# Edge lists with room in steps of 32, list sums from signs, and attention sums divided on ScalarE, in a four-layer graph network

## The chip, the cores and the metric

One core of one Trainium2 chip. The metric is the device time of one execution in microseconds (us), the median of several. All runs compared were in the fast state of their chip (one of the 20 runs of x_less_pe0 was slow and is left out; f_before is a single run, whose state can't be told, but its 1780.26 us is within 0.3 us of the median of the 16 runs of the same kernel beside it, 1780.51). The chips themselves differ, though, and this matters throughout: the kernel before takes about 1780 us on some (called **quick chips** here) and 1940 to 1960 us on others (**slow chips**). So runs are compared only with runs of the kernel before on the same chip. A ratio is the mean time of one kernel's fast runs over that of the other's of the same rounds, so it is not quite the ratio of the medians that are quoted; brackets give its 95% interval.

## The reference

3327 nodes with 512 features, an adjacency matrix (ones with probability falling with both node numbers, so early rows are heavy), and four layers, each followed by a residual addition and a layer norm:

```python
x = _layernorm(x + _L0_gnn_ref(x, adj, W, a1, a2))       # graph attention, 8 heads of 64, softmax over neighbours, elu
x = _layernorm(x + _L1_gnn_ref(x, adj, ...))             # mean of the neighbours' x, three 512x512 products, relu
x = _layernorm(x + _L2_gnn_ref(x, adj, ...))             # mean of the first 64 neighbours, two products, leaky relu
x = _layernorm(x + _L3_gnn_ref(x, adj, W, a))            # attention, 4 heads of 128 (quaternion weights)
```

## The kernel before

The engines' names in the profiles: PE is TensorE's matmuls, PEld its weight loads, DVE VectorE, ACT ScalarE, POOL GpSimd. The kernel never multiplies with the dense matrix (apart from block 0 in the mean layers). It makes a list of the edges of each block of 128 nodes, in chunks of 128 edges. Each layer then gathers the source rows of a chunk with one indirect DMA issued by GpSimd (a **gather**; its rows land in a ring of buffers), and TensorE adds them into the block's sum with a 0/1 selection matrix. Cut to what the change touches:

```python
CAPS = (0, 19, 15, 13, 11, 10, 10, 9, 9, 8, 8, 7, 7, 7, ...)     # chunks of 128 per block's list
...
    step = const.tile([P, P], F32, name="step")                   # difference of neighbours, for the list sums
    nc.vector.tensor_copy(step, ident)
    nc.vector.tensor_sub(step[:, 1:], ident[:, 1:], ident[:, :P - 1])
...
                    u = mid.tile([P, g * P], BF16, name="u")      # list sums: place >= start, then a product with dl
                    nc.vector.tensor_scalar(u, place[:, c0 * P:(c0 + g) * P], start, None, ALU.is_ge)
...
    def gather(ring, table, l, c0, g):
        t = ring.take(g)
        for c in range(g):
            nc.gpsimd.indirect_dma_start(
                out=t[:, c, :], out_offset=None, in_=table[:, :],
                in_offset=bass.IndirectOffsetOnAxis(ap=l.idx[:, c0 + c:c0 + c + 1], axis=0))
        return t
...
            for c in range(g):                                    # attention layers 0 and 3, one group of chunks
                for s in range(2):
                    nc.tensor.matmul(accs[b][s], S[:, c, :], G[:, c, s * hh * M:(s + 1) * hh * M],
                                     start=at + c == 0, stop=at + c == chunks_of[b] - 1)
...
            for s in range(2):                                    # end of a block: attention sum / its weight
                nc.vector.tensor_mul(h[:, s], acc[s][:, :, :OUT], rden[:, s].to_broadcast([P, hh, OUT]))
...
            for k in range(3):                                    # mean layers 1 and 2: three bf16 parts of a row
                nc.tensor.matmul(accs[b], S[:m, c, :], G[:m, c, k * D:(k + 1) * D],
                                 start=at + c + k == 0, stop=k == 2 and at + c == n - 1)
```

## Time and profile before

| | us |
|---|---|
| time before, median of 3 runs (quick chip) | 1779.0 (1775.2 to 1780.38) |
| span of the profile of before that the prediction read | 1940.1, mean granted clock 0.927 |

The second row was on hand and I only scaled it away: the profile was of a slow chip (the profiled execution itself took 1941.98 us), the times of a quick one. The granted clock is the share of TensorE's full clock that the throttle let through. The prediction shows the profile's lines. A profile of the kernel before on a quick chip came with the experiments (run f_before, 1780.26 us), and it is the one to compare with the kernel after. Its first line of busy time and shares, then busy us (instructions) of PE, PEld, DVE, ACT, POOL by stage, granted clock, DMA share and GB/s. The stages are: before layer 0, layer 0, layer 1, block 0 of layer 2, the rest of layer 2, layer 3 without its first and last groups.

```profile
PE 1565.7 (88%) x8167; PEld 1027.4 (58%) x8215; DVE 1286.9 (72%) x3269; ACT 668.4 (38%) x1964; POOL 975.7 (55%) x1061
...
0.00:231.00 231.00, 183.73 (x1046) 136.00 (x1047) 189.22 (x693) 116.21 (x447) 24.79 (x37) 0.94 0.53 176
231.00:699.00 468.00, 430.54 (x2691) 312.55 (x2691) 435.23 (x1103) 245.38 (x585) 269.84 (x298) 0.95 0.73 232
699.00:1069.00 370.00, 367.08 (x1300) 173.70 (x1323) 211.49 (x429) 71.53 (x136) 223.35 (x230) 1.00 0.86 297
1069.00:1146.00 77.00, 69.83 (x228) 33.17 (x230) 34.32 (x60) 13.46 (x29) 21.56 (x29) 0.98 0.54 197
1146.00:1403.00 257.00, 234.06 (x1054) 141.01 (x1074) 127.90 (x312) 66.45 (x326) 194.12 (x193) 0.99 0.94 324
1430.00:1762.00 332.00, 261.10 (x1741) 217.56 (x1741) 272.46 (x616) 140.04 (x390) 238.92 (x272) 0.95 0.75 216
```

What to see, against the stages in the prediction: the instructions are the same (the trace of f_before lacks the records of 48 matmuls, 8167 against 8215), yet TensorE has far less idle time. In layer 1 it idles 3 of 370 us (18 to 21 of 394 to 397 in the slow chip's profile); over the whole span it idles 213 us against 314.

### The profile page before, as it was taken

The numbers are of one execution on the slowest core, as the hardware profiler recorded it, in microseconds if no ns is written. First come the engines' busy times: TensorE is split into PE (matmuls) and PEld (weight loads), VectorE is DVE, ScalarE is ACT, GpSimd is POOL, SyncE is SP. The second block draws the span as 40 slices with busy tenths as digits, with TensorE's granted clock in tenths as the row PEclk, the third lists the DMA queues.
The fourth block names the chain that finished last, engine by engine and source line by source line (L and its number), as shares of the span: only waits on it lengthen the run. The fifth ranks groups of instructions, "written<-read, shape, count | busy, mean of one in ns | idle before, by whom it ended". The sixth has DMA issues, their size and how long they took to land.

```text
span 1940.1 us, 25543 instructions
## 1 busy us (share of the span) xinstructions
PE 1626.2 (84%) x8215; PEld 1055.9 (54%) x8215; DVE 1286.1 (66%) x3269; ACT 666.7 (34%) x1964; POOL 970.9 (50%) x1061
## 2 busy tenths in 40 slices
PE   5999477888889999998899999688888568778775
PEld 4667366655566774443444444355555456566654
DVE  8897489988988883135567864633434336677887
ACT  3365344545544553211111121122222313333443
POOL 1000455544455643637665532666666266666660
PEclk9899688989999999999999999898898889898998
DMA  8434667766765757968888873888888366666771
GB/s 268 149 116 151 205 200 256 255 221 215 237 178 177 220 161 254 310 215 294 271 314 284 284 279 130 284 278 293 294 297 275 91 184 186 192 203 197 205 210 61
DMA packets 125148, 431.38 MB, mean 222 GB/s; under 512 B 25294, under 2 KB 26830, under 8 KB 125004
## 3 DMA queue, kind: packets, MB, share of 16 engines
q0 software_dynamic: 76480, 314.26, 52.1%
q1 hardware_dynamic: 48524, 115.40, 17.0%
q8 instruction: 67, 1.10, 0.2%
q14 instruction: 77, 0.63, 0.1%
HBM read 381.54 MB, written 48.04 MB: 221 GB/s over the span
## 4 chain that ended last, share of the span: by engine, by line
PE 61%; DVE 22%; issue 10%; DMA 2%; ACT 2%; another core or an unknown queue 2%; POOL 1%; SPq 0%; DVEq 0%; ACTq 0%; POOLq 0%
PE po L742 17%; PE acc L1077 15%; PE acc L1351 14%; PE po L965 7%; DVE gt L1070 4%; DVE cand L854 3%; PE pt L727 2%; PE pg L1050 2%; DMA gt<-t_d,idx 2%; DVE cand L868 1%; DVE sl L866 1%; DVE st L747 1%; DVE val L836 1%; DVE e L1099 1%
## 5 line engine op out<-in xcount | busy, mean ns | idle before, releaser
L934 POOL DMA_INDIRECT gt<-t_d,idx x788 | 788.3, 1000 | 726.9 <-ACT g0own L788 201.9
L1077 PE MATMUL acc<-gt,sel 128*128 128x264 f32 (+1 forms) x1828 | 484.4, 414 | 52.9 <-issue 26.1
L1077 PEld LDWEIGHTS acc<-gt,sel 128*128 128x128 f32 x1828 | 357.5, 203 | 139.4 <-issue 80.4
L1070 DVE TENSOR_TENSOR gt<-gt,pg 128x1536 f32<-128x1536 f32 (+1 forms) x137 | 263.2, 1921 | 10.7 <-ACT sel L1065 4.6
L742 PE MATMUL po<-wn,xt 128*128 128x512 f32 x416 | 201.5, 629 | 20.9 <-ACT xt L730 11.1
L934 POOL DMA_INDIRECT gx<-t_d,idx x116 | 116.5, 1004 | 63.1 <-issue 27.2
L965 PE MATMUL po<-w,xt 128*128 128x262 f32 x416 | 112.5, 431 | 36.1 <-issue 32.7
L742 PEld LDWEIGHTS po<-wn,xt 128*128 128x128 f32 x416 | 81.2, 202 | 110.3 <-issue 92.5
L1062 ACT ACTIVATE pg<-sc 128x24 f32<-128x24 f32 (+4 forms) x148 | 28.1, 190 | 301.1 <-DVE sc L1061 162.5
L1351 PE MATMUL acc<-gt,sall 128*128 128x512 bf16 x498 | 118.7, 388 | 8.4 <-issue 8.2
L854 DVE MAX8 cand<-val 128x8 f32<-128x832 uint16 (+40 forms) x259 | 125.6, 524 | 0.0
L965 PEld LDWEIGHTS po<-w,xt 128*128 128x128 f32 x416 | 88.2, 215 | 61.0 <-issue 38.5
L1050 PEld LDWEIGHTS <-ds 128*128 128x128 bf16 x1482 | 64.2, 99 | 92.6 <-issue 47.0
L1351 PE MATMUL acc<-gt,sel 128*128 128x512 bf16 x495 | 114.0, 379 | 0.0
L965 PE MATMUL po<-gt,xt 128*128 128x268 f32 x416 | 104.3, 400 | 2.8 <-ACT xt L734 2.6
L1351 PEld LDWEIGHTS <-sall 128*128 128x128 fp8e4 x615 | 61.1, 100 | 83.8 <-issue 22.0
L730 ACT COPY xt<-pt 128x512 f32<-128x512 f32 x86 | 50.6, 589 | 152.6 <-PE pt L727 90.3
L1351 PEld LDWEIGHTS <-sel 128*128 128x128 bf16 x615 | 60.2, 98 | 78.5 <-issue 17.3
L742 PE MATMUL po<-wx,xt 128*128 128x512 f32 x208 | 97.2, 610 | 5.6 <-issue 2.5
L1038 ACT ACTIVATE far<-place,nmid 128x384 int16<-128x384 int16 (+2 forms) x148 | 94.8, 644 | 20.4 <-DVE ds L1042 13.0
L727 PE MATMUL pt<-s_ident,xres 128*128 128x128 f32 x520 | 80.1, 278 | 21.2 <-DMA xres<-in_x_dram 16.0
L742 PE MATMUL po<-wl,xt 128*128 128x512 f32 x208 | 94.0, 594 | 2.9 <-issue 1.5
(230 smaller groups left out, 2465.6 us busy)
## 6 DMA issues: line engine op xcount, KB each, us to landing
ab<-in_adj_dram SPq DMA_DIRECT2D x25, 832.0 KB
ab<-in_adj_dram SPq DMA_DIRECT2D x25, 831.5 KB
t_d<-t SPq DMA_DIRECT2D x50, 384.0 KB
gt<-t_d POOLq DMA_DIRECT2D x42, 384.0 KB
gt<-t_d,idx POOLq DMA_INDIRECT x788
t_d<-tg SPq DMA_DIRECT2D x25, 264.0 KB
t_d<-tg SPq DMA_DIRECT2D x25, 260.0 KB
xres<-in_x_dram SPq DMA_DIRECT2D x25, 256.0 KB
```

The source lines that it names most:

```text
L727: nc.tensor.transpose(pt[:, c, :], src[:, c * P:(c + 1) * P], ident)
L730: nc.scalar.copy(xt, pt)
L742: nc.tensor.matmul(po, xt[:, c, :], w[:, c], start=c == 0, stop=c == DC - 1)
L854: nc.vector.max(out=top, in_=seg)
L934: nc.gpsimd.indirect_dma_start(out=t[:, c, :], out_offset=None, in_=table[:, :], in_offset=bass.IndirectOffsetOnAxis(ap=l.idx[:, c0 + c:c0 ...
L965: nc.tensor.matmul(pw[s], xt[:, c, :], self.w[:, c, s, :], start=c == 0, stop=c == DC - 1)
L1038: nc.scalar.activation(far[:, :g * P], place[:, c0 * P:(c0 + g) * P], AF.Abs, bias=l.nmid, scale=2.0)
L1050: nc.tensor.matmul(pe[:, c], ds[:, c * P:(c + 1) * P], self.own[:, k, :, b], start=k == 0, stop=k == 2)
L1062: nc.scalar.activation(w[:, :g], sc[:, :g, 0], AF.Exp)
L1070: nc.vector.tensor_mul(Gc[:, :, :OUT], Gc[:, :, :OUT], w[:, :g].rearrange("p c (h o) -> p (c h) o", o=1).to_broadcast([P, g * H, OUT]))
L1077: nc.tensor.matmul(accs[b][s], S[:, c, :], G[:, c, s * hh * M:(s + 1) * hh * M], start=at + c == 0, stop=at + c == chunks_of[b] - 1)
L1351: nc.tensor.matmul(accs[b], S[:m, c, :], G[:m, c, k * D:(k + 1) * D], start=at + c + k == 0, stop=k == 2 and at + c == n - 1)
```

## The change

Intent: (1) give each list room in multiples of 32 edges instead of 128, so that 4 of 247 chunks go and many last gathers bring 32, 64 or 96 rows; group sizes are fitted to the end of the ring; (2) take the comparison behind the list sums off VectorE by a sign activation on ScalarE; (3) do the division of the attention sums on ScalarE, head by head.

```diff
-CAPS = (0, 19, 15, 13, 11, 10, 10, 9, 9, 8, 8, 7, ...)
+CAPS = (0, 2368, 1856, 1568, 1376, 1280, 1152, 1088, 1024, 992, 928, 896, ...)
...
+        L = self.L = -(-room // P)
+    def places(self, c):
+        return min(P, self.room - c * P)
...
+    def ahead(self):                                  # class Ring
+        return self.parts[self.part].shape[1] - self.at
...
-    nc.vector.tensor_copy(step, ident)
-    nc.vector.tensor_sub(step[:, 1:], ident[:, 1:], ident[:, :P - 1])
+    nc.vector.tensor_scalar(step, ident, 0.5, None, ALU.mult)
+    nc.vector.scalar_tensor_tensor(step[:, 1:], ident[:, :P - 1], -0.5, step[:, 1:], ALU.mult, ALU.add)
+    nc.vector.scalar_tensor_tensor(step[:, 0:1], ident[:, P - 1:], 0.5, step[:, 0:1], ALU.mult, ALU.add)
...
+                nc.scalar.activation(here, p1[:, 0:1], AF.Identity, bias=point5, scale=-1.0)
...
-                    nc.vector.tensor_scalar(u, place[:, c0 * P:(c0 + g) * P], start, None, ALU.is_ge)
+                    nc.scalar.activation(u, place[:, c0 * P:(c0 + g) * P], AF.Sign, bias=here)
...
-                for k in range(n):
-                    g = l.L // n + (k < l.L % n)
+                while c0 < l.L:
+                    left = l.L - c0
+                    g = -(-left // -(-left // GROUP))
+                    if 1 < ring.ahead() < g:
+                        g = ring.ahead()
...
-                out=t[:, c, :], ... ap=l.idx[:, c0 + c:c0 + c + 1]
+                out=t[:m, c, :], ... ap=l.idx[:m, c0 + c:c0 + c + 1]          # m = l.places(c0 + c)
...
+            for p0 in range(m, P, 32):                # attention: zero the scores of rows not gathered
+                nc.scalar.copy(G[p0:p0 + 32, g - 1]...[:, :, OUT:], zeros[p0:p0 + 32, :2 * H]...)
...
-                    nc.tensor.matmul(accs[b][s], S[:, c, :], G[:, c, s * hh * M:(s + 1) * hh * M],
+                    nc.tensor.matmul(accs[b][s], S[:m, c, :], G[:m, c, s * hh * M:(s + 1) * hh * M],
...
-                nc.vector.tensor_mul(h[:, s], acc[s][:, :, :OUT], rden[:, s].to_broadcast([P, hh, OUT]))
+                for k in range(hh):
+                    nc.scalar.activation(h[:, s, k], acc[s][:, k, :OUT], AF.Identity, scale=rden[:, s, k])
```

Cut: the same for the heavy lists of block 0, the constants that the sign form needs, the arguments that pass the ring, the row counts in the mean layers.

More of the change, by code (lines that the diff above doesn't have):

```diff
@@ L524, in general_path @@
     gat("l3", xs_d[2], out, l3_w.shape[0], l3_w.shape[2], l3_weights, False)
-HEAVY = ((0, 9, 14, 120, 9, 3), (9, 18, 14, 120, 9, 3), (18, 27, 14, 120, 9, 3))
-CAPS = (0, 19, 15, 13, 11, 10, 10, 9, 9, 8, 8, 7, 7, 7, 7, 7, 6, 6, 6, 6, 6, 6, 6, 6, 5, 5)
+HEAVY = ((0, 9, 1760, 120, 9, 3), (9, 18, 1792, 120, 9, 3), (18, 27, 1792, 120, 9, 3))
+CAPS = (0, 2368, 1856, 1568, 1376, 1280, 1152, 1088, 1024, 992, 928, 896, 864, 832, 800, 768, 768, 736, 704,
+        704, 672, 672, 672, 640, 640, 608)
 SLOTS = (0, 48, 40, 40, 32, 32, 32, 32, 32) + (24,) * 17
@@ L544, with __init__ @@
 class EdgeList:
-    def __init__(self, pool, name, cuts, L, K, rounds, at):
-        self.cuts, self.L, self.K, self.rounds, self.at = cuts, L, K, rounds, at
+    def __init__(self, pool, name, cuts, room, K, rounds, at):
+        self.cuts, self.room, self.K, self.rounds, self.at = cuts, room, K, rounds, at
+        L = self.L = -(-room // P)
         self.idx = pool.tile([P, L], U32, name=f"idx{name}")
@@ L646, in sparse_path @@
         lists.append([])
-        for q, (s0, s1, L, K, n, rounds) in enumerate(parts):
+        for q, (s0, s1, room, K, n, rounds) in enumerate(parts):
             cuts = [int(NP * ((s0 + (s1 - s0) * s / n) / total) ** 2) // 2 * 2 for s in range(n + 1)]
             cuts = [c for i, c in enumerate(cuts) if i in (0, n) or c >= 8 * rounds]
-            lists[b].append(EdgeList(keep, f"{b}_{q}", cuts, L, K, rounds, sum(map(len, lists)) - 0))
+            lists[b].append(EdgeList(keep, f"{b}_{q}", cuts, room, K, rounds, sum(map(len, lists)) - 0))
     NL = sum(map(len, lists))
@@ L680, in sparse_path @@
     pos = iota("pos", LMAX, I16, P, 0, 1)
+    zeros = const.tile([P, 16], F32, name="zeros")
+    nc.gpsimd.memset(zeros, 0.0)
     eps = const.tile([P, 1], F32, name="s_eps")
@@ L692, in sparse_path @@
     step = const.tile([P, P], F32, name="step")
-    nc.vector.tensor_copy(step, ident)
-    nc.vector.tensor_sub(step[:, 1:], ident[:, 1:], ident[:, :P - 1])
+    nc.vector.tensor_scalar(step, ident, 0.5, None, ALU.mult)
+    nc.vector.scalar_tensor_tensor(step[:, 1:], ident[:, :P - 1], -0.5, step[:, 1:], ALU.mult, ALU.add)
+    nc.vector.scalar_tensor_tensor(step[:, 0:1], ident[:, P - 1:], 0.5, step[:, 0:1], ALU.mult, ALU.add)
     dls = [const.tile([P, 2, KMAX + 2], BF16, name=f"dl{k}") for k in range(2)]
     for dl in dls:
-        for s in range(2):
-            nc.gpsimd.memset(dl[:, s, 0:1], 1.0 - s)
+        nc.gpsimd.memset(dl[:, 0, 0:1], 0.5)
+        nc.gpsimd.memset(dl[0:1, 0, 0:1], 0.5 + P / 2)
+        nc.gpsimd.memset(dl[:, 1, 0:1], 0.0)
+    point5 = const.tile([P, 1], F32, name="point5")
+    nc.gpsimd.memset(point5, 0.5)
     H0, _, OUT0 = l0_w.shape
@@ L880, in structure @@
                 nc.tensor.matmul(p1[:, 1:2], middle, dg, start=True, stop=True)
+                here = mid.tile([P, 1], F32, name="here")
+                nc.scalar.activation(here, p1[:, 0:1], AF.Identity, bias=point5, scale=-1.0)
                 nc.scalar.copy(start, p1[:, 0:1])
@@ L916, in structure, with groups @@
             yield b
-    def groups(blocks=range(NB)):
+    def groups(ring, blocks=range(NB)):
         for b in blocks:
@@ L922, in groups @@
             for l in lists[b]:
-                n = -(-l.L // GROUP)
                 c0 = 0
-                for k in range(n):
-                    g = l.L // n + (k < l.L % n)
+                while c0 < l.L:
[3 more added lines that the diff above has]
+                        g = ring.ahead()
                     yield b, l, c0, g, at
@@ L933, in gather @@
         for c in range(g):
+            m = l.places(c0 + c)
             nc.gpsimd.indirect_dma_start(
-                out=t[:, c, :], out_offset=None, in_=table[:, :],
-                in_offset=bass.IndirectOffsetOnAxis(ap=l.idx[:, c0 + c:c0 + c + 1], axis=0))
+                out=t[:m, c, :], out_offset=None, in_=table[:, :],
+                in_offset=bass.IndirectOffsetOnAxis(ap=l.idx[:m, c0 + c:c0 + c + 1], axis=0))
         return t
@@ L1035, in group @@
             G = gather(ring, self.table, l, c0, g)
+            m = l.places(c0 + g - 1)
+            for p0 in range(m, P, 32):
+                nc.scalar.copy(G[p0:p0 + 32, g - 1].rearrange("p (h m) -> p h m", m=M)[:, :, OUT:],
+                               zeros[p0:p0 + 32, :2 * H].rearrange("p (h s) -> p h s", s=2))
             far = sp.tile([P, GROUP * P], I16, name="far")
@@ L1075, in group @@
             for c in range(g):
+                m = l.places(c0 + c)
                 for s in range(2):
-                    nc.tensor.matmul(accs[b][s], S[:, c, :], G[:, c, s * hh * M:(s + 1) * hh * M],
+                    nc.tensor.matmul(accs[b][s], S[:m, c, :], G[:m, c, s * hh * M:(s + 1) * hh * M],
                                      start=at + c == 0, stop=at + c == chunks_of[b] - 1)
@@ L1286, in sparse_path @@
     w2lay = ExitStack()
-    for item in groups():
+    for item in groups(pools[0]):
         b = item[0]
@@ L1348, in mean_group @@
         for c in range(g):
-            m = LAST if b == 0 and c0 + c == NB - 1 else P
+            m = LAST if b == 0 and c0 + c == NB - 1 else P if b == 0 or sall else l.places(c0 + c)
             for k in range(3):
@@ L1427, in own_part @@
             nc.vector.tensor_add(xres[b], xi, xres[b])
-        for items in (first_items(), groups(range(1, NB))):
+        for items in (first_items(), groups(ring, range(1, NB))):
             for item in items:
@@ L1504, in layer2_end @@
             g3.write(b, fin, pw)
-        for item in groups(mixed()):
+        for item in groups(ring, mixed()):
             work.add(mean_group(item, t2_d, near0, lambda b, acc: ends.add(layer2_end(b, acc)), sall))
@@ L1546, in verdict @@
                 for l in ls:
-                    nc.gpsimd.memset(room[:, l.at:l.at + 1], float(l.L * P))
+                    nc.gpsimd.memset(room[:, l.at:l.at + 1], float(l.room))
             yield
@@ L1560, in sparse_path @@
         ends.add(verdict())
-        for item in groups():
+        for item in groups(pools[0]):
             work.add(g3.group(item, pools, accs, layer3, sall))
```

## The prediction

> **What bounds the kernel now.** I began with the page's busy shares, then cut the span into the kernel's stages (by first and last start of the lines that belong to each layer) and asked the busy time of each engine in each stage; shares over the whole span mix stages with different limits.
>
> ```profile
> PE 1626.2 (84%) x8215; PEld 1055.9 (54%) x8215; DVE 1286.1 (66%) x3269; ACT 666.7 (34%) x1964; POOL 970.9 (50%) x1061
> ...
> 0.00:211.00 211.00, 177.74 (x945) 129.61 (x945) 176.35 (x649) 105.75 (x419) 8.73 (x22) 0.96 0.51 168
> 211.00:592.00 381.00, 301.45 (x1955) 221.63 (x1956) 325.06 (x859) 178.34 (x435) 205.28 (x210) 0.87 0.70 224
> 592.00:743.00 151.00, 148.25 (x839) 103.54 (x837) 123.15 (x290) 77.30 (x179) 79.85 (x103) 1.00 0.63 189
> 743.00:1140.00 397.00, 376.23 (x1322) 175.88 (x1320) 212.34 (x431) 71.69 (x137) 223.07 (x232) 0.97 0.83 280
> 1217.00:1525.00 308.00, 259.82 (x1128) 160.51 (x1127) 130.24 (x320) 72.65 (x365) 188.66 (x191) 0.91 0.81 268
> 1550.00:1940.00 390.00, 283.42 (x1727) 226.47 (x1725) 274.31 (x625) 141.94 (x391) 230.05 (x235) 0.91 0.63 180
> ```
>
> Below the first line the columns are start:end, length, then busy us (instructions) of PE, PEld, DVE, ACT, POOL, then granted clock, DMA share, GB/s. Rows: projections and first lists; layer 0 while lists are still built; layer 0 after that; layer 1; layer 2; layer 3. Layer 0's first part is VectorE's (325 of 381 us, 85%, PE 79%). Its second part and layer 1 are TensorE's (98% and 95%). Layer 2 has PE at 84% with transfers at 81% and 268 GB/s. Layer 3 has no full engine (PE 73%, DVE 70%, POOL 59%): a pipeline of groups in which each engine waits for the next.
>
> Next the chain of work that ended last, inside layer 0's first part and inside layer 2:
>
> ```profile
> by line: PE acc L1077 23.8%; issue 11.2%; PE po L742 10.8%; DVE gt L1070 8.8%; DVE cand L854 8.3%; DMA gt<-t_d,idx 5.2%; DVE val L836 3.6%; PE pg L1050 3.0%; PE pg L1056 2.1%; PE pv L900 1.3%; DVE ds L1042 1.3%; another core or an unknown q
> ...
> by line: PE acc L1351 44.9%; PE po L965 36.0%; issue 14.8%; PE pt L727 3.5%; ACT tg L976 0.4%; ACT xt L734 0.4%; PE pmean L990 0.2%; ACT g3fall L977 0.0%; ACTq L734 0.0%
> ```
>
> In the first, PE and DVE lines alternate: work moves between two nearly full engines. In the second only PE is named, but 14.8% (46 us) is "issue", a wait the profile can't name; PE's longest ones there (8.3 us) stand before work that needs gathered rows or their products. I read them as late gathers, which is an inference.
>
> Last, the rows of what the change touches:
>
> ```profile
> L934 POOL DMA_INDIRECT gt<-t_d,idx x788 | 788.3, 1000 | 726.9 <-ACT g0own L788 201.9
> L1093 DVE TENSOR_TENSOR h<-acc,rden 128x256 f32<-128x256 f32 x104 | 39.5, 417 | 1.0
> L895 DVE TENSOR_SCALAR u<-place,starts x41: 231/406/611, 47.5 to 583.8; 128x512 bf16<-128x512 int16 x9, 128x768 bf16<-128x768 int16 x8, 128x1280 bf16<-128x1280 int16 x6, 128x896 bf16<-128x896 int16 x5
> L802 ACT ACTIVATE xres<-e,nm,rs x26: 797/813/821, 356.7 to 745.7; 128x512 f32<-128x512 f32 x26
> ```
>
> A gather of 128 rows costs POOL 1.0 us; the division of the attention sums 0.417 us of DVE, 104 times; the comparison behind the list sums 17 us of DVE in all. The last row calibrates an ACT operation with two per-row operands.
>
> **What the Trainium skill says.** "ScalarE: Activation LUTs", What ACT_TABLE_LOAD costs: an ACTIVATE takes 186 ns + 0.833 ns per element, 93 ns more for each per-partition operand, and neighbours overlap by 93 ns. For 512 elements and two operands that is 799 ns; the trace has 797 to 821. "VectorE: DVE Perf Modes", The perf-mode tier table: two-tensor operations with a PSUM source run at 1x, single-source 16-bit ones up to 4x. The trace agrees: 0.417 us for 256 elements against 0.6 us for 1280. So the comparison is cheap where it stands and dear on ACT. "TensorE: Matmul & The Clock Gate", LDWEIGHTS: the time goes with the columns, not with the contraction rows, so short chunks should save PE nothing; before, the 127-row matmuls took the same 377 to 382 ns as the 128-row ones. "DMA: Bandwidth & Descriptors", Why a DMA increments its semaphore by 16 and not by 1: row counts that are multiples of 16 spread over all 16 engines. 32, 64 and 96 are; no run yet shows a short gather here.
>
> **Part 1: room in steps of 32.** Counted from the diff: 247 chunks become 243 (lists 6, 8, 15 and 23 lose one each). Rows gathered fall from 31,616 to 29,952 in layers 0 and 3 (-5.3%), and from 26,240 to 24,608 in layers 1 and 2 (-6.2%), where block 0 is dense. 888 gathers instead of 904: POOL loses 16 us plus whatever short gathers save. PE, per attention layer: 4 chunks x (4 passes x 0.265 us [262.0 us of L1077 over 988 passes] + 3 score passes x 0.048 + one 0.11 us transpose) = 5.3 us; per mean layer 12 passes x 0.23 = 2.8 us. DVE: 4 x 0.6 us per attention layer. Transfers: 1,632 rows x 3,072 B = 5.0 MB less in each mean layer, at layer 2's 268 to 288 GB/s some 17 to 19 us of transfer time. The rings are also filled to their end: by replaying the two groupings, slots skipped at the wrap go from 25 to 7 in layers 1 and 2, 25 to 5 in layer 3, 11 to 4 in layer 0, so gathers start earlier. Against that, 2 more groups (3 in layer 3), each about 0.6 us of fixed DVE time in attention layers, and 36 small zeroing copies on ACT per attention layer (36 x 0.17 = 6 us), on an engine that has room.
>
> **Part 2: signs on ACT.** DVE loses 17.2 us: 7.6 us before 211 us and 9.6 us in layer 0's first part. ACT gains 41 x (280 + 0.833 x 771) ns = 38 us (247 chunks x 128 / 41 = 771 elements each) and 28 x 0.27 us for the new biases.
>
> **Part 3: division on ACT.** DVE loses 19.8 us in layer 0 (8.4 in its first part, 11.5 in the second) and 19.7 us in layer 3. ACT gains, with the overlap, 26 x 8 x 0.24 = 50 us in layer 0 and 26 x 4 x 0.29 = 31 us in layer 3. ACT in layer 0 goes from 256 of 532 us to about 335 (63%), in layer 3 from 36% to 46%: not a bound, but per block the step to the exponential grows from 0.76 to about 1.9 us in layer 0, 1.2 us in layer 3.
>
> **Sum, in us of the profile.** Before 211: -3, since DVE and PE share the path and DVE loses 7.6. Layer 0, first part: DVE loses about 20 of 325, PE at 79% can follow for about 60% of it: -12. Second part: PE-bound, so the 11.5 us of DVE is idle time; only PE's savings count: -2. Layer 1: 2.8 us of PE and a few of the 21 us that PE idles: -6. Layer 2: half of the transfer time, since transfers are the limit in its first half only: -10. Layer 3: 0.76 us leaves a DVE queue whose next entry is the scaling that PE waits for, in 26 of 74 steps (20 us), with 5 us of PE; about 40% arrives: -9. Together -42 of 1940. Timed runs are 1779, so scaled by 0.917: -38, or **1740 us**.
>
> **Rivals.** (a) *PE takes the place of DVE and of the transfers*: PE is busy 84% of the span, and 95% and more in two stages. Then only PE's 16 us and little idle time come out: about 1762. The full rows of layer 1 speak for it; layers 2 and 3 with 16% and 27% PE idle against. (b) *ACT becomes the new wait*: its queue is in order, a block's eight scalings stand ahead of the next group's exponential and selection copy, and zeroing waits for a ring slot. The trace has DVE waiting for ACT's list copies already (some 20 us in layer 0). This would eat layer 0's gain and make 1755 to 1775. ACT's share of under half speaks against. (c) *Gathers are the main limit of layers 2 and 3*: "issue" of 46 us in layer 2 and POOL's 1.26 us from gather to gather (0.95 busy + 0.30) speak for it. Then fewer rows and better-filled rings save 15 to 20 us in each of layers 1 to 3, and the time is near 1715. The 28 us that POOL spends in layer 2 waiting for stores of the layer before speak against: those stay.
>
> **Range and chances.** Rival (c) in part and (a) in part span the range: 1710 to 1767. The 2% line is 1743.4, only 3 us above my figure, so faster is 0.54. Within 2% is 0.43: rivals (a) and (b) both end there. Slower by over 2% needs ACT to stall the whole pipeline or the lists not to fit and the general path to run: 0.03.
>
> **What would show it right or wrong.** Right: layer 0's first part shorter by about 12 us with DVE's share lower and PE's higher; layer 2 shorter by about 10 us with less "issue"; L1093 gone from DVE, ACT rows of 208 and 104 instructions near 0.33 and 0.39 us; short gathers moving fewer bytes; PE passes of short chunks as long as the others. Wrong: PE waits on ACT's division or zeroing lines; layer 2 as long as before though 6% fewer rows came in (then transfers were not its limit); layer 1 much shorter (then its PE share hid waits); layer 3 unchanged although DVE lost 20 us.

## The result, and the profile after

| | us |
|---|---|
| before, median of 4 runs | 1779.69 (1775.2 to 1782.32) |
| after, median of 4 runs | 1761.91 (1756.43 to 1763.67) |
| ratio | 0.9897 [0.9867, 0.9928] |

The gain is 1.0%, 18 us, where I had forecast 38. It lies within the range of 1710 to 1767 and on the "within 2%" side of the line. The kernel after by the same stages as above:

```profile
PE 1558.2 (89%) x8076; PEld 1013.0 (58%) x8123; DVE 1233.5 (70%) x3144; ACT 781.9 (44%) x2437; POOL 949.1 (54%) x1049
...
0.00:226.00 226.00, 183.01 (x1043) 134.59 (x1044) 181.84 (x672) 130.85 (x473) 22.26 (x38) 0.94 0.52 173
226.00:688.00 462.00, 424.69 (x2657) 305.69 (x2655) 406.07 (x1036) 307.68 (x877) 260.04 (x289) 0.96 0.70 225
688.00:1061.00 373.00, 367.63 (x1287) 170.44 (x1310) 212.75 (x431) 73.18 (x139) 220.00 (x236) 1.00 0.85 289
1061.00:1137.00 76.00, 70.03 (x229) 33.17 (x230) 34.33 (x60) 13.45 (x29) 21.33 (x29) 0.98 0.55 199
1137.00:1389.00 252.00, 227.70 (x1044) 139.99 (x1064) 127.66 (x312) 66.56 (x326) 189.90 (x189) 0.99 0.91 310
1415.00:1741.00 326.00, 265.78 (x1713) 215.63 (x1712) 255.39 (x578) 172.78 (x534) 232.82 (x269) 0.93 0.73 210
```

Stage by stage (before to after): 231 to 226, 468 to 462, 370 to 373, 77 to 76, 257 to 252, 332 to 326 us. Nothing gave what I had put on it, and layer 1 gave nothing. The work itself changed as counted: VectorE lost 53 us of busy time, ScalarE gained 114 (busy time counts overlaps once; VectorE's summed durations fell by 62), and 888 gathers stand in place of 904. The durations were as worked out. The groups by line of the kernel after, with nanoseconds as least/median/most:

```profile
L1124 ACT ACTIVATE h<-acc,rden x312: 291/344/388, 310.7 to 1748.0; 128x64 f32<-128x64 f32 x104, 128x128 f32<-128x128 f32 x52
...
L915 ACT ACTIVATE u<-place,here x41: 403/952/1492, 47.8 to 524.9; 128x512 bf16<-128x512 int16 x9, 128x768 bf16<-128x768 int16 x8, 128x1280 bf16<-128x1280 int16 x5, 128x640 bf16<-128x640 int16 x4
...
L1063 ACT COPY gt<-zeros x68: 193/201/205, 165.4 to 1725.9; 32x16 f32<-32x16 f32 x36, 32x8 f32<-32x8 f32 x32
...
L1383 PE MATMUL acc<-gt,sel x472: 373/379/387, 747.4 to 1061.1; 128*128 128x512 bf16 x141, 64*128 64x512 bf16 x6, 32*128 32x512 bf16 x6, 96*128 96x512 bf16 x5
...
L958 POOL DMA_INDIRECT gt<-t_d,idx x769: 862/946/2851, 209.3 to 1720.2; - x193
```

The divisions took 291 to 388 ns (worked out: 0.33 and 0.39 us); matmuls of 32, 64 or 96 rows took the same 373 to 387 ns as those of 128; and a short gather costs GpSimd hardly less than a whole one: the least is 862, the median 946 ns. So the parts were sized right as work. What went wrong is how much of the work stood on the path.

### The profile page after: what moved, and what is told of

It is laid out like the page before. It is cut to its first block, busy times and chain, and to the rows that moved or that the text cites. A ratio compares the mean times of both kernels' runs of the same rounds, so it can differ in the third digit from the quotient of the medians.

```text
span 1759.3 us, 25652 instructions
## 1 busy us (share of the span) xinstructions
PE 1558.2 (89%) x8076; PEld 1013.0 (58%) x8123; DVE 1233.5 (70%) x3144; ACT 781.9 (44%) x2437; POOL 949.1 (54%) x1049
## 4 chain that ended last, share of the span: by engine, by line
PE 56%; DVE 17%; DMA 13%; ACT 5%; issue 5%; POOL 3%; SPq 0%; DVEq 0%; POOLq 0%; ACTq 0%
PE po L760 19%; PE acc L1383 13%; PE acc L1107 12%; DMA gt<-t_d,idx 9%; PE po L989 6%; DMA gx<-t_d,idx 4%; DVE gt L1099 3%; DVE cand L872 3%; PE pt L745 2%; POOL gt L958 2%; DVE sl L884 1%; DVE cand L886 1%; PE pg L1079 1%; ACT h L1124 1%; DVE st L765 1%
## 5 line engine op out<-in xcount | busy, mean ns | idle before, releaser
L958 POOL DMA_INDIRECT gt<-t_d,idx x769 | 769.8, 1001 | 594.0 <-ACT vc L923 202.0
L1107 PE MATMUL acc<-gt,sel 128*128 128x264 f32 (+5 forms) x1776 | 458.3, 407 | 37.6 <-issue 16.2
L1107 PEld LDWEIGHTS acc<-gt,sel 128*128 128x128 f32 (+3 forms) x1776 | 338.4, 199 | 112.0 <-issue 48.8
L1099 DVE TENSOR_TENSOR gt<-gt,pg 128x1536 f32<-128x1536 f32 (+3 forms) x138 | 256.2, 1856 | 15.0 <-ACT sel L1094 13.5
L958 POOL DMA_INDIRECT gx<-t_d,idx x119 | 117.5, 987 | 42.3 <-issue 18.3
L872 DVE MAX8 cand<-val 128x8 f32<-128x832 uint16 (+39 forms) x259 | 126.3, 522 | 0.1
L1383 PE MATMUL acc<-gt,sel 128*128 128x512 bf16 (+2 forms) x472 | 112.6, 379 | 0.7
L1091 ACT ACTIVATE pg<-sc 128x24 f32<-128x24 f32 (+5 forms) x153 | 29.2, 191 | 185.4 <-DVE sc L1090 164.2
L1383 PEld LDWEIGHTS <-sel 128*128 128x128 bf16 (+3 forms) x603 | 57.8, 97 | 80.1 <-issue 22.7
L1067 ACT ACTIVATE far<-place,nmid 128x384 int16<-128x384 int16 (+3 forms) x153 | 96.7, 634 | 8.8 <-DVE ds L1071 8.5
L745 PEld LDWEIGHTS pt<-s_ident,xres 128*128 128x128 f32 x520 | 64.2, 143 | 50.0 <-issue 31.1
```

The source lines that it names most:

```text
L745: nc.tensor.transpose(pt[:, c, :], src[:, c * P:(c + 1) * P], ident)
L872: nc.vector.max(out=top, in_=seg)
L958: nc.gpsimd.indirect_dma_start(out=t[:m, c, :], out_offset=None, in_=table[:, :], in_offset=bass.IndirectOffsetOnAxis(ap=l.idx[:m, c0 + c: ...
L1067: nc.scalar.activation(far[:, :g * P], place[:, c0 * P:(c0 + g) * P], AF.Abs, bias=l.nmid, scale=2.0)
L1091: nc.scalar.activation(w[:, :g], sc[:, :g, 0], AF.Exp)
L1099: nc.vector.tensor_mul(Gc[:, :, :OUT], Gc[:, :, :OUT], w[:, :g].rearrange("p c (h o) -> p (c h) o", o=1).to_broadcast([P, g * H, OUT]))
```

## The experiments

Eighteen kernels ran. The first twelve fell on slow chips, the last six on quick ones, where the answer lies; a chip can't be chosen.

### On slow chips: the parts alone, and the whole without one

First, is the gap between 1779 and 1940 us a disturbed execution, the cost of profiling, or the chip? The kernel before, unchanged:

> The kernel before, unchanged, for a second profile. The profile that the prediction was read from spans 1940 us though the timed runs take 1779; the changed kernel's profile spans 1759 us for timed runs of 1762. Theory A (the first profile was of a disturbed execution): this profile spans 1775 to 1785 us with a granted clock near 0.96, and layer 2's and layer 3's unnamed waits shrink by most of the 161 us. Rival B (profiling costs this kernel 9%): it spans 1930 us or more again.

It took 1958.15 us (ratio 0.9997 [0.9981, 1.0013]) and its profile spans 1955.2 us: the profile costs nothing and nothing was disturbed. This chip runs the kernel slower, every time.

Each part alone, put into the kernel before:

```diff
# d_only_divide: only the division of the diff above;  s_only_signs: only step, here, Sign, dl and point5
# r_only_rooms: the kernel after with those two undone
```

> Only the division moved to ACT. My prediction's steps put about 5 us on layer 0's first part and about 8 us on layer 3: ratio near 0.993. Rival (ACT becomes the wait): 1.000 to 1.005, with PE or DVE waiting for the division's lines. Rival (PE is the bound of what is left): 0.998.

> Only the list sums' signs moved to ACT. Prediction's steps: 3 us before 211 us and 6 us in layer 0's first part, ratio 0.995. Rival: the 0.95 us on ACT lengthens the chain of a list by half a microsecond 41 times and delays copies that PE waits for, ratio 1.000 to 1.005.

> Only the rooms in steps of 32, with short gathers, zeroing and filled rings. Prediction's steps: 2 us in layer 0, 6 in layer 1, 10 in layer 2, 2 in layer 3: ratio 0.989. If transfers were the main limit (rival c): 0.975. If PE bounds what is left: 16 us of PE work at most, ratio 0.991 or more, with layer 2 hardly shorter than its PE savings of 2.8 us.

Then the kernel after and each part undone in it (n_no_rooms is signs and division in the kernel before):

> The changed kernel, unchanged, timed beside before on this chip. The first timing gave 0.990 on a chip where before takes 1779 us; on the chip of the first four runs (before 1958 us) the three parts alone gave 1.005, 1.003 and 0.996. Theory C (the parts add up, and chips differ in what limits them): on a chip of 1958 us this gives 1.000 to 1.006, on one of 1779 us 0.990. Rival D (the parts need each other): 0.990 on either.

> The changed kernel with the division back on DVE. If moving the division costs by itself (as alone, +0.5%), this is 0.5% faster than the changed kernel, and layer 0 ends about 10 us earlier. If it pays only once the signs have also left DVE, this is 0.3 to 0.7% slower than the changed kernel.

> The changed kernel with the list sums' comparison back on DVE. If moving it costs by itself (as alone, +0.3%), this is 0.3% faster than the changed kernel. If the prediction's step holds beside the other parts (9 us), it is 0.5% slower.

> Signs and division on ACT, rooms and gathers as before. Additive: 1.008 of before on a chip of 1958 us, layers 1 to 3 as before to 3 us, layer 0 longer by some 25 us. If rooms carry the whole gain on a chip of 1779 us: 1.000 or more there.

Measured. Stages as above; layer 3 is counted here from the last selection of layer 2 to its last sum.

| run | ratio | layer 0 | layer 1 | layer 2 | layer 3 |
|---|---|---|---|---|---|
| b0_before | 0.9997 [0.9981, 1.0013] | 494 | 398 | 304 | 419 |
| d_only_divide | 1.0052 [1.0036, 1.0068] | 508 | 402 | 303 | 420 |
| s_only_signs | 1.0034 [1.0021, 1.0047] | 505 | 396 | 304 | 418 |
| r_only_rooms | 0.9964 [0.9936, 0.9993] | 510 | 386 | 298 | 419 |
| a_after | 1.0025 [1.0, 1.005] | 507 | 392 | 302 | 422 |
| n_no_divide | 1.001 [0.9989, 1.003] | 508 | 389 | 300 | 422 |
| n_no_signs | 0.9983 [0.9967, 0.9999] | 503 | 388 | 300 | 421 |
| n_no_rooms | 1.0041 [1.0015, 1.0068] | 501 | 400 | 307 | 420 |

On a slow chip the whole change gains nothing, and signs and division, which take the most from VectorE, cost 0.3 to 0.5% each. The parts roughly add (0.52 + 0.34 - 0.36 = 0.50% for a measured 0.25 +- 0.25). Every variant has a layer 0 that is 7 to 16 us longer than b0_before's, however its work moves (two more slow-chip profiles with an unchanged layer 0, those of the prediction and of d3_only below, have 499 and 493 us, so the lower end is within what profiles differ); the room shortens layer 1 by 6 to 12 us and layer 2 by 2 to 6, and nothing shortens layer 3. So next, does VectorE or TensorE set layer 0 at all? Take work from each alone (results wrong on purpose), and try the parts where they might still help: the division in layer 3 only, and the room with layer 0 gathering whole chunks and zeroing nothing.

```diff
# x_less_dve0: two VectorE operations per block less in layer 0
-            nc.vector.scalar_tensor_tensor(hq, hq, 0.0, xb, ALU.max, ALU.add)
-            nc.vector.scalar_tensor_tensor(e, e, 1.0, hq, ALU.min, ALU.add)
+            if self.k:
+                nc.vector.scalar_tensor_tensor(hq, hq, 0.0, xb, ALU.max, ALU.add)
+                nc.vector.scalar_tensor_tensor(e, e, 1.0, hq, ALU.min, ALU.add)
# x_less_pe0: one product less at the end of ten blocks of layer 0
-        nc.scalar.copy(zb, times(ps, xt, wx))
+        nc.scalar.copy(zb, x1)
# d3_only
+                if self.k == 0:
+                    nc.vector.tensor_mul(h[:, s], ...)      # as before
+                    continue
# r_13, in r_only_rooms
-            m = l.places(c0 + c)
+            m = P if table is t0_d else l.places(c0 + c)
```

> Wrong result on purpose: the kernel before without the two 0.69 us VectorE operations that make ELU and residual in layer 0 (52 operations, 36 us of DVE in layer 0, nothing else taken away). If VectorE bounds layer 0, as the prediction said, layer 0 shortens by 15 to 30 us and the time by 1 to 1.5%. If TensorE and what holds it bound layer 0 (DVE fell by 27 us in the changed kernel and layer 0 did not shorten), it shortens by less than 5 us: ratio 0.998 to 1.003.

> Wrong result on purpose: the kernel before without the product with wx at the end of 10 blocks of layer 0 (10 x 8 passes of 0.43 us = 34 us of TensorE; ACT copies as many bytes from elsewhere). If TensorE bounds layer 0, it shortens by 25 to 34 us: ratio 0.983 to 0.987. If VectorE does, by less than 12 us, that is the part of the ten products that lies after list building: ratio above 0.994.

> Only the division of layer 3 on ACT; layer 0's stays on DVE. The prediction put 8 of its 9 us there: ratio 0.995. On the profiles of the first chip layer 3 takes 389 us before and 390 with the division moved, so if that holds, 1.000, and the 0.5% loss of the division alone is layer 0's.

> The rooms alone, but layer 0 gathers its last chunks whole and zeroes nothing; layers 1 to 3 as with the rooms. Rooms alone had layer 0 longer by 16 us in one profile and layers 1 and 2 shorter by 18. If the zeroing copies and short gathers cost that, layer 0 ends near 742 and the ratio is 0.989. If it is the order of work or the smaller groups, it stays as it was, 0.996.

Measured: 0.9993 [0.997, 1.0017], 1.0008 [0.9985, 1.0031], 0.9991 [0.9973, 1.0009], 0.9972 [0.995, 0.9993]. On a slow chip relief of neither engine shows, so neither alone sets layer 0. What does, I could not settle. The division in layer 3 alone (the third) gained nothing of its forecast 0.5%. In r_13 layer 0 takes 499 us, as long as an unchanged one, where r_only_rooms had 510; so short gathers and zeroing may lengthen layer 0 on a slow chip, but the ratio of r_13 is no better. The traces show where the time goes: summing the gaps of over 0.55 us between the starts of neighbouring matmuls gives 399 us in b0_before and 231 us in f_before, a difference of 168 us, near the 177 us between the spans. But such a gap includes the matmul that opens it: by busy time TensorE idles 339 against 213 us, 127 of the 177, and the other 50 are longer busy times. What holds TensorE there, the trace doesn't name.

### On quick chips: before, the room, and the other two parts

> The kernel before, unchanged, for a profile on this chip. If the chip is of the quicker kind: about 1780 us, and stages near those of the changed kernel there (layer 0 462, layer 1 373, layer 2 252, layer 3 352 us) with some 18 us more in sum. My theory (transfers and TensorE give the gain, VectorE's relief nothing): layer 1 longer by 8 to 12 us, layer 2 by 3 to 8, layers 0 and 3 within 5. The rival (VectorE's relief arrives when TensorE isn't held up): layer 0 or 3 longer by 8 us or more. On a slower chip: 1940 to 1960 us and the stage table known already.

> The room in steps of 32 alone. On a quicker chip, if the room gives the whole gain: ratio 0.987 to 0.992. If VectorE's relief gives half of it: 0.994 to 0.997. On a slower chip it gave 0.9964 before.

> Signs and division on ScalarE without the room. On a quicker chip, if VectorE's relief gives nothing: 0.998 to 1.003. If it gives half of the gain: 0.992 to 0.996. On a slower chip it gave 1.0041 before.

| run | median, us | ratio | gain, us |
|---|---|---|---|
| f_rooms | 1770.9 | 0.9942 [0.9924, 0.996] | 10.3 |
| f_no_rooms (signs and division) | 1774.33 | 0.9959 [0.9946, 0.9973] | 7.3 |
| both: the change | 1761.91 | 0.9897 [0.9867, 0.9928] | 18.3 |

The gain is one minus the ratio, times the median before (1780.5; for the last row 1779.7). Here the parts add up in time. The room gives 10 us of a forecast 18 (its terms -2, -6, -10 and 2 of layer 3's 9, times 0.917), signs and division 7 of a forecast 20 (-3, -12, -7 times 0.917). My expectation "the room alone gives it all" fell as well as its rival: each gives about half. By stage, the room shows in layers 2 and 3 (4 and 6 us); signs and division show in 2 us before layer 0 and 3 us of layer 3:

```profile
233.00:702.00 469.00, 424.28 (x2676) 302.81 (x2675) 432.49 (x1114) 253.60 (x632) 257.80 (x288) 0.97 0.69 219
...
1147.00:1400.00 253.00, 230.00 (x1045) 140.52 (x1065) 126.82 (x312) 66.46 (x326) 189.74 (x189) 0.99 0.92 308
...
1427.00:1753.00 326.00, 261.09 (x1713) 212.54 (x1713) 272.52 (x628) 149.32 (x438) 232.44 (x268) 0.95 0.73 209
```

```profile
229.00:698.00 469.00, 433.24 (x2693) 313.48 (x2692) 411.72 (x1031) 303.13 (x838) 268.74 (x302) 0.95 0.73 235
...
1427.00:1756.00 329.00, 265.96 (x1741) 220.91 (x1741) 256.34 (x566) 164.64 (x489) 241.98 (x272) 0.93 0.76 218
```

The first fence is f_rooms (layers 0, 2 and 3: 253 and 326 us in the last two, as in the kernel after), the second f_no_rooms (layers 0 and 3). In f_no_rooms VectorE loses 23.5 us in layer 0 (435.23 to 411.72) and the layer stays at 469 us.

Two cautions. The 2 and 3 us of signs and division are no more than what kernels differ by that are unchanged there: f_before and the three wrong-on-purpose kernels below have 228 to 233 us before layer 0, and 329 to 332 in layer 3. So where their 7 us arise is not shown. And by stage the parts do not add up: layer 0 takes 469 us with either part, 468 before, and 462 with both. These are single profiles, and why it should shorten only with both, no run shows.

### On quick chips: which engine sets layer 0

The two kernels that take work from one engine, again, now here:

> The kernel before without two VectorE operations per block in layer 0 (36 us of VectorE; wrong on purpose). My theory now (both engines over 90% full, each only partly in the way): about a quarter of it arrives, 6 to 12 us, ratio 0.993 to 0.997, layer 0 at 457 to 463 us. The prediction's step (60% of VectorE's relief arrives): 20 us, ratio 0.988. If TensorE alone is the bound: 1.000 within 0.002. On a slower chip: 0.9993 was measured.

> The kernel before without the product with wx that stands at the end of ten blocks of layer 0 (34 us of TensorE; wrong on purpose). If TensorE bounds layer 0: 25 to 34 us, ratio 0.981 to 0.986. If both engines share it: 8 to 15 us, ratio 0.991 to 0.996. If VectorE or the order of the work bounds it: 1.000 within 0.002, as the slower chip had (1.0008).

```profile
228.00:688.00 460.00, 426.63 (x2694) 310.47 (x2693) 406.43 (x1053) 245.55 (x586) 268.75 (x302) 0.96 0.75 237
```

```profile
233.00:696.00 463.00, 402.22 (x2620) 302.55 (x2616) 432.54 (x1108) 244.87 (x586) 267.67 (x299) 0.93 0.74 234
```

f_less_dve0 (first fence, layer 0): 0.9943 [0.9929, 0.9956], 10.2 us for 29.0 us less of VectorE's busy time (1286.9 to 1257.9 over the whole span; the durations taken out sum to the 36 I had counted, but busy time counts overlaps once), so 35% arrives. The two operations also stand in the chain that ends a block, so part of it may be that chain. f_less_pe0 (second): 0.9959 [0.9946, 0.9972], 7.3 us for 29.9 us less of TensorE (1565.7 to 1535.8), so 24%. Neither engine alone is the bound: each relief arrives by a quarter to a third. That fits my later theory that both stand in the way by turns (the 7.3 us lie just under its 8 to 15), and not the 60% of the prediction; no run took work from both at once.

### On quick chips: what sets layer 2

The prediction took layer 2's limit to be transfers. This kernel gathers 96 rows of each 128-row chunk there:

```diff
+        m = 96 if table is t2_d else P
-                out=t[:, c, :], ... ap=l.idx[:, c0 + c:c0 + c + 1]
+                out=t[:m, c, :], ... ap=l.idx[:m, c0 + c:c0 + c + 1]
```

> The kernel before, gathering 96 rows instead of 128 of each chunk in layer 2, and in the four groups of it gathered ahead (wrong on purpose): about 20 MB less, TensorE unchanged. If transfers bound layer 2 until TensorE does: layer 2 shorter by 12 to 20 us (257 to about 240 on the quicker chip), ratio 0.989 to 0.993. If the bound is the issue of gathers or the latency of each, which do not go with rows: shorter by under 4 us, ratio over 0.998.

Measured: 0.9953 [0.994, 0.9966], 8.4 us; layer 2 went from 257 to 251 us. Between the two expectations, so neither held, and small: a quarter less of gathered data gave what 6% less (the room) had given. The transfer part of each trace for layer 2, f_before and then x_rows2 (GB/s, then per queue packets, MB and the share of the 16 transfer engines):

```profile
DMA packets 18990, 83.19 MB, mean 324 GB/s; under 512 B 3521, under 2 KB 3521, under 8 KB 18974
...
q0 software_dynamic: 15648, 76.87, 87.2%
```

```profile
DMA packets 15858, 63.95 MB, mean 255 GB/s; under 512 B 3521, under 2 KB 3521, under 8 KB 15842
...
q0 software_dynamic: 12516, 57.63, 84.1%
```

The gathers (q0) moved 19 MB less, yet filled the transfer engines 84% of the time instead of 87%. Each packet took longer: 16 engines x 257 us x 0.872 / 15,648 = 229 ns before, 16 x 251 x 0.841 / 12,516 = 270 ns here. So a high share of busy transfer engines was not a full pipe. What does set the stage is in GpSimd's lines. Count, busy us, mean ns, then us idle just before them; layer 2 of f_before, of x_rows2 and of the kernel after:

```profile
L934 POOL DMA_INDIRECT gt<-t_d,idx x158 | 159.2, 1008 | 48.1 <-issue 18.9 <-PE acc L1351 11.9 <-PE po L965 6.7
L934 POOL DMA_INDIRECT gx<-t_d,idx x35 | 35.8, 1024 | 10.7 <-issue 3.4 <-PE acc L1351 3.4 <-DMA gt<-t_d,idx 1.8
```

```profile
L935 POOL DMA_INDIRECT gt<-t_d,idx x157 | 152.4, 971 | 47.8 <-issue 19.8 <-PE acc L1352 9.1 <-DMA gt<-t_d,idx 7.6
L935 POOL DMA_INDIRECT gx<-t_d,idx x35 | 35.8, 1024 | 10.7 <-issue 4.9 <-PE acc L1352 2.1 <-DMA gt<-t_d,idx 1.8
```

```profile
L958 POOL DMA_INDIRECT gt<-t_d,idx x155 | 156.9, 1012 | 47.2 <-issue 18.0 <-PE acc L1383 13.4 <-DMA gt<-t_d,idx 7.0
L958 POOL DMA_INDIRECT gx<-t_d,idx x34 | 33.8, 994 | 10.4 <-issue 4.0 <-PE acc L1383 2.7 <-PE po L989 2.1
```

Sum busy and idle of both lines: 253.8 of 257 us, 246.7 of 251, 248.3 of 252. The idle time is 58.8 us over 193 gathers, 0.305 us each, and no single one is longer: the waits of GpSimd in layer 2 of f_before are headed by

```profile
POOL gt L934 <- issue: 18.9, 62, 0.3
POOL gt L934 <- PE acc L1351: 11.9, 39, 0.3
```

(us in total, times, longest). So GpSimd never waits for a free buffer: it issues one gather after the other from end to end, mostly 0.95 us of work (1.01 in the mean) and 0.3 us between, as the timeline has it (start, length, idle before):

```profile
1300.61 0.95 POOL L934 DMA_INDIRECT gt<-t_d,idx  x1 [0.30 <-issue]
1301.86 0.95 POOL L934 DMA_INDIRECT gt<-t_d,idx  x1 [0.30 <-issue]
```

**Layer 2 on a quick chip is bound by the issue of gathers, and is about as long as their number times 1.31 us** (1.28 with 96 rows: the issue does go a little with rows, 5.9 us of GpSimd's busy time in all, which is why my "under 4 us" failed). Against f_before the sums are less by 7.1 us (x_rows2) and 5.5 us (after), the stages by 6 and 5. Could full transfers hold up the issue? All that the gathers of f_before take above the shortest one, 0.95 us, sums to 11 us, so no more than that. And the room alone could not tell this bound from TensorE, whose busy time in layer 2 falls by the same 4 us; x_rows2, with the same TensorE instructions as before, can (its busy time falls by 4 us there too, presumably because part of what counts as busy had been waiting).

Layer 3 is nearly the same, by its traces; no run tested it by itself. Its lines in f_before, in the kernel after, and in the slow chip's profile of before:

```profile
L934 POOL DMA_INDIRECT gt<-t_d,idx x207 | 202.2, 977 | 63.2 <-issue 23.5 <-PE acc L1077 17.7 <-DMA gt<-t_d,idx 11.3
L934 POOL DMA_INDIRECT gx<-t_d,idx x37 | 36.0, 974 | 11.3 <-issue 4.9 <-DMA gt<-t_d,idx 1.5 <-PE acc L1077 1.5
```

```profile
L958 POOL DMA_INDIRECT gt<-t_d,idx x199 | 191.7, 963 | 60.7 <-issue 27.5 <-PE acc L1107 12.2 <-DMA gt<-t_d,idx 9.1
L958 POOL DMA_INDIRECT gx<-t_d,idx x42 | 41.1, 979 | 12.8 <-issue 6.7 <-PE acc L1107 3.0 <-DMA gx<-t_d,idx 1.5
```

```profile
L934 POOL DMA_INDIRECT gt<-t_d,idx x204 | 199.2, 977 | 98.6 <-issue 44.6 <-PE acc L1077 20.8 <-remote 9.3
L934 POOL DMA_INDIRECT gx<-t_d,idx x37 | 36.8, 995 | 17.8 <-issue 7.9 <-PE pg L1050 4.1 <-PE acc L1077 3.8
```

312.7 of 332 us in f_before and 306.3 of 326 in the kernel after: 6.4 us less, and the stage is 6 us shorter. (The missing 20 us is the tail after the last gather.) The room takes out 4 gathers in each of these two layers; 8 x 1.3 = 10.4 us, and it gained 10.3 (that they agree so closely is luck: the interval of the ratio runs from 7 to 14 us, and layers 0 and 1 lost gathers too, without getting shorter). On the slow chip GpSimd has real waits in layer 3 (0.48 us before each gather), and layer 3 stayed at 419 us with the room alone. That the waits are why is an inference: layer 2 of that profile has 0.48 us too, and there the room gained 2 to 6 us.

No version was best on both kinds of chip: the change as a whole is the best measured on quick chips, the room alone on slow ones (0.9964), and the room is the only part that gained on both.

## Why the prediction was wrong

It forecast -38 us and 18 came; the direction held. Three of its steps failed: the share of VectorE's relief that arrives in layer 0, the idle time of TensorE that layer 1 was to give back, and transfers as the limit of layer 2. By its own steps, with the forecast scaled by 0.917 as it says and the measured stages of f_before and after:

| step | forecast, us | measured, us | verdict |
|---|---|---|---|
| before layer 0 | -3 | -5 | held in sign; profiles of unchanged code differ by 5 us there |
| layer 0, both parts | -13 | -6 | too high, and in neither part alone |
| layer 1 | -6 | +3 | failed |
| layer 2 | -9 | -5 | right sign, wrong mechanism |
| layer 3 | -8 | -6 | about right in size, for another reason |

**Layer 0: "DVE loses about 20 of 325, PE at 79% can follow for about 60% of it: -12."** This is the largest term; its miss of 7 us comes next after layer 1's 9. Taking 29 us from VectorE and adding nothing elsewhere gave 35% (f_less_dve0). With signs and division the 23.5 us taken from VectorE in layer 0 gave nothing there that one profile can show. The 79% came from a slow chip, and from a stretch that began before layer 0's sums; in f_before, from the first sum to the end of list building (231 to 551 us), TensorE is busy 89% and VectorE 97%. What takes the rest of the relief stays open. Moving the work to ScalarE may cost part of what it brings (f_less_dve0 gained 10.2 us with less relief than f_no_rooms, which gained 7.3, but the intervals overlap), and no run added ScalarE's work without the relief. No run held the order of the work fixed either.

**Layer 1: "2.8 us of PE and a few of the 21 us that PE idles."** Those 21 us were the slow chip's. On a quick chip TensorE idles 3 of 370 us, so there was nothing to give back but the removed passes. Even these don't show: the layer came out at 371 (f_rooms) and 373 us (after), against 369 or 370 in the profiles without the room. The traces show one reason: a pass normally starts 0.22 us after the one before it, so 12 passes are 2.6 us, but the first pass on a chunk of 32 or 64 rows starts after 0.31 us (12 times in f_rooms, 1.2 us). What takes the rest isn't shown. On slow chips, where there was idle time, the room did shorten it: 386 to 392 us with it, 396 to 402 without.

**Layer 2: "half of the transfer time, since transfers are the limit in its first half only."** Transfers are not the limit: 19 MB less gained 6 us. The limit is GpSimd's issue, 1.31 us per gather and hardly less when it brings fewer rows; 4 gathers gave the 5 us. The forecast had the number for it ("0.95 busy + 0.30" in rival (c)), and listed 16 gathers fewer as POOL's own saving, but didn't multiply: 193 x 1.31 is 253 us. Rival (c) had the right cause and the wrong size, since it counted rows, which cost little here, and ring slots, for which GpSimd never waits in layers 2 and 3, beside the gathers.

**Layer 3: "0.76 us leaves a DVE queue ... about 40% arrives: -9"**, with "no full engine (PE 73%, DVE 70%, POOL 59%)". POOL was the full engine on the timed chip: the page does not count the 0.3 us between gathers as busy. The step itself, less VectorE work in front of TensorE, is not shown to have gained anything: signs and division alone give 329 us, as does f_less_pe0, whose layer 3 is unchanged. By the lines above, the 6 us are the fewer gathers, as in layer 2.

**The scaling.** One step stands behind several: "Timed runs are 1779, so scaled by 0.917." The 9% is not a common factor. Layer 0 after list building takes 151 us there and 148 in f_before. Of the 162 us between the spans 101 are idle time of TensorE (314 against 213 us), and I had counted parts of that idle time as room for gains. A profile whose span is 9% over the timed runs is not a profile of those runs.

**Right:** the durations on ScalarE, short passes as long as the others, the counts, and that ScalarE would not be full. But a sign that the prediction named for being wrong did come, if small: TensorE waits for the division's lines, 4.0 us in 5 waits in the kernel after, and VectorE's wait for the exponential behind the division grew from 10.5 us (f_before) to 25.5. Rival (a), "TensorE takes the place", ended at 1762 and so met the number; its cause holds for layer 1 alone. Rival (b), ScalarE as the new wait, had 1755 to 1775 and met it as well; these waits are its cause, and how much of the missing gain they are is not shown.

**Open:** what makes slow chips slow (their mean granted clock is lower too, 0.92 to 0.93 against about 0.96, and no run separates that from the rest), why signs and division cost time there, what takes the rest of their relief on quick chips, and why neither engine's relief shows in layer 0 there.

## What to carry to other kernels

Check first that the profile is of the same speed as the timed runs; idle time that only the profile has is not there to be won. Ask of a stage with many gathers how many there are times the distance from one start to the next, not how busy the engine or the transfers are: here a stage at "POOL 76%" and "transfers 94%" was bound by the issue of gathers, so fewer gathers pay and smaller ones hardly do. And where two engines are both nearly full, don't count on most of the relief of one: here a quarter to a third of it arrived.

## What the Trainium skill lacked or had wrong

- "DMA: Bandwidth & Descriptors", Issuing engines are not separate DMA queues, says that the time it takes to initiate a DMA "is usually small relative to the DMA itself". 128-row indirect gathers of 3 KB rows are an exception, since here it bounds the stage: 1.31 us from one to the next on GpSimd, 253.8 of 257 us of layer 2, while a quarter less data gained 6 us.
- The same page, SWDGE vs HWDGE vs iDMA, says that GpSimd computes the descriptors in software but gives no time from one indirect gather to the next. Here most gathers took 0.91 us at 96 rows against 0.95 to 0.96 at 128 in layer 2, 0.862 us at the least for any short gather, and another 0.30 us passed between neighbours, which a busy share leaves out.
- No page read for this case says that chips differ this much: the same kernel took 1780 us on some and 1940 to 1960 us on others, with the same median durations of single operations and 127 us more of idle TensorE (b0_before against f_before).
